# Mixer input of the 512-token segments: loaded by feature and normalised in place, instead of normalised by token and turned on TensorE

## The chip, the cores and the metric

The kernel runs on one core of one Trainium2 chip. The metric is device time in microseconds (us) of that core for one launch; three runs of the kernel before are given. All arithmetic on the path that matters here is float32.

A reminder of the engines, in the names that the profile uses: PE is TensorE (its weight loads are listed as PEld), DVE is VectorE, ACT is ScalarE, POOL is GpSimd, SP is SyncE, which here issues DMAs. Each engine executes its own list of instructions strictly in order, and an instruction that waits holds up everything behind it on that engine.

## The reference, cut to what matters

The input is four sequences of 1024 tokens with 256 features. A Mamba-2 mixer and a gated feed-forward block follow each other, each with a layer norm in front of it and behind it:

```python
x = x + _layernorm(_mamba2_forward(_layernorm(x), ...))      # x: (4, 1024, 256)
x = x + _layernorm(_ffn(_layernorm(x), ...))

def _layernorm(x, axis=-1, eps=1e-05):
    m = jnp.mean(x, axis=axis, keepdims=True)
    v = jnp.var(x, axis=axis, keepdims=True)
    return (x - m) / jnp.sqrt(v + eps)

# inside the mixer the first use of its input u = _layernorm(x) is
zxbcdt = u @ in_proj_kernel          # (256 -> 1288): z, xBC and dt
```

The change concerns only the first layer norm, that of the mixer's input, and the form in which it reaches the first product. TensorE contracts over partitions, so that product wants the normalised input with its 256 features on partitions and the tokens along the row.

## The kernel before, in words

**Segments.** The tokens are cut into nine segments, `SEGS`: the first 256 and the next 256 tokens of sequence 0 (segments 0 and 1), then the first 512 tokens of sequences 1 to 3 (segments 2 to 4), then the last 512 tokens of all four sequences (segments 5 to 8). For each segment `mixer(s)` gives a list of steps (`norm_in`, `step_sizes`, `features` or `feature_pair`, `decays`, `gate` or `gate_pair`, and for every chunk of 128 tokens `inner`, `scan`, `gated`, `way_out`, `turned`), and `ffn(s)` gives those of the feed-forward block. From segment 2 on (feed-forward) and segment 4 on (mixer, `SEVEN`) the large products are done as seven half-size products on sums of operands.

**Order.** Nothing is issued directly. A `Recorder` notes each operation as a step with its operands, the bytes that it reads and writes and an estimated duration (`weigh`). `Recorder.issue` then plays the whole program through, engine by engine, with due times: of the steps whose inputs and buffers are due it takes the one with the lowest rank (`rank`), and writes the instructions in that order. So the order of all engines follows from estimates made on the host, and a changed step moves others far away from it. A small DMA (under 20,000 bytes) is due 1900 ns after its issue there, a large one by its bytes; whatever another engine takes from a DMA is planned 1500 ns later still (`LATE_DMA`).

**Buffers.** `pools` hands out slots by name. What matters here: `x` (input rows by token, three slots), `xn` (one chunk of normalised rows, two slots), `xnT` (the normalised input by feature, 128 partitions x 2 x 512, a single slot), `th` (128 x 512, three slots, otherwise used for the tanh in the convolution), `a`, `f` and `d` (banks of PSUM, where products land), `mvm` (mean and variance per token) and `rsm` (the reciprocal standard deviation).

**The step that is changed.** `norm_in` has the rows of the segment in `x`, 128 tokens on partitions, four chunks. DVE takes `bn_stats` and `bn_aggr` of each chunk; POOL makes (variance + eps) to the power of -0.5 in two instructions (`rstd_of`). Then for each chunk DVE writes (x - mean) * rstd into `xn`, and PE turns its two halves of 128 features with a product against the identity into two banks. Two copies on ACT move the banks to `xnT`. Those lines are:

```python
for i in range(NC):
    xn = get("xn")
    r.vector.tensor_scalar(xn, x[:, i, :], mv[:, i, 0:1], rs[:, i : i + 1], ALU.subtract, ALU.mult)
    for kk in range(2):
        r.tensor.transpose(pT[kk][:, i * P : (i + 1) * P], xn[:, kk * P : (kk + 1) * P], ident)
for kk in range(2):
    r.scalar.copy(xnT[:, kk, :], pT[kk][:, :T])
```

**What comes behind it.** `step_sizes` is the first reader of `xnT` on PE (eight small products with `dtw`), `input_sums` takes sums of its quarters on DVE (segments 4 to 8), `feature_pair` and `gate_pair` read it to the end of the mixer's projections. `pair` puts two results into two `f` banks, and `convolve` then reads each of them with one ACT instruction and three DVE instructions (the taps) before the bank is free again.

**DMA traffic next to it.** All large DMAs go through SP's one queue: the feed-forward weights in blocks of 1792 KB (`wide<-stock`, `fetch`), the mixer's weights of 448 KB (`win<-mstock`), decays that are written to DRAM and read back for many partitions at once (`rows<-cst`, then `e<-rows` and `r<-rows`), rows of the input (`x<-in_u`) and of the output (`out_dram<-fo`).

Of the kernel before, what the change touches and what calls it, by code (L numbers as in the profile page):

```python
# [14 lines left out]
ALU = mybir.AluOpType  # L15
PSUM = bass.MemoryType.PSUM

P = 128
EPS = 1e-5
NB, L, DM = 4, 1024, 256  # L20
DI, NH, HD, DS = 512, 8, 64, 128
# [7 lines left out]
CMAX = TMAX // P  # L29
# [376 lines left out]
def mamba_ffn_kernel(  # L406
    ctx: ExitStack,
    tc: tile.TileContext,
    u: bass.AP,
    w_in: bass.AP,  # L410
    conv_w: bass.AP,
    conv_b: bass.AP,
# [13 lines left out]
    r = Recorder(tc.nc)  # L426
    sb = ctx.enter_context(tc.tile_pool(name="sb", bufs=1))
    psum = ctx.enter_context(tc.tile_pool(name="psum", bufs=1, space=PSUM))
    hbm = ctx.enter_context(tc.tile_pool(name="hbm", bufs=1, space=bass.MemoryType.DRAM))

    def pool(name, shape, k=1, ahead=2, of=None, dtype=F32):
        of = of or sb
        return Pool([of.tile(shape, dtype, name=f"{name}{j}") for j in range(k)], ahead)

    def fixed(name, shape, dtype=F32):
        return pool(name, shape, dtype=dtype).get()

    def given(ap):
        return Pool([ap]).get()

    u, w_in, conv_w, conv_b, dt_bias, a_log, d_skip, norm_w, w_out = map(
        given, (u, w_in, conv_w, conv_b, dt_bias, a_log, d_skip, norm_w, w_out))
    g_pack, g_scale, u_pack, u_scale, d_pack, d_scale, out = map(
        given, (g_pack, g_scale, u_pack, u_scale, d_pack, d_scale, out))

# [9 lines left out]
        "yo": pool("yo", [P, DI // P, P]), "xf": pool("xf", [P, 2, P], 2),  # L455
        "xfT": pool("xfT", [P, 2, TMAX], 2), "act": pool("act", [P, HALF], 3, 3),
        "fo": pool("fo", [P, DM], 2), "cst": pool("cst", [CMAX * NH, P], 2),
        "rows": pool("rows", [CMAX * NH, P], 2, of=hbm), "dec": pool("dec", [P, 3 * CMAX * NH], 2),
        "edge": pool("edge", [P, NF, 3], 2), "part": pool("part", [P, NF, 3], 2),
        **{k + who: pool(k + who, shape, 4, 4) for who in "mf"  # L460
           for k, shape in (("mv", [P, CMAX, 2]), ("st", [P, 6]), ("rs", [P, CMAX]))},
# [5 lines left out]
    def get(tag):  # L467
        return pools[tag].get()


    def rows_of(s):
        b, t0, T = SEGS[s]
        return b * L + t0, T
# [3 lines left out]
    def by_segment(s, tag, cut):  # L477

        if s > 1:
            return cut(get(tag), slice(0, SEGS[s][2]))  # L480
        if tag not in shared:
            shared[tag] = get(tag)
        return cut(shared[tag], slice(SEGS[s][1], SEGS[s][1] + SEGS[s][2]))

    xs = {}
# [11 lines left out]
    def load_win(c0, c1, queue=r.sync):  # L497
# [8 lines left out]
                     in_=w_in[:, DPROJ - NH :].rearrange("(k p) m -> p k m", p=P))  # L506
# [3 lines left out]
    for name, shape, src in (("dtb", [P, NH], dt_bias), ("aneg", [P, NH], a_log),  # L510
                             ("cw", [P, NF, 4], conv_w), ("cb", [P, NF], conv_b),
                             ("dsk", [P, DI // P], d_skip), ("nw", [P, DI // P], norm_w)):
        t = small_loads[name] = fixed(name, shape)
# [14 lines left out]
    mhalf = fixed("mhalf", [P, CMAX])  # L528
# [55 lines left out]
    def little(tag, n):  # L584
        return get(tag)[:, :n]

    def rstd_of(var, n, factor=1.0):

        v = get("rsm")[:, :n]
        r.gpsimd.tensor_scalar(v, var, factor, EPS * factor, ALU.mult, ALU.add)  # L590
        r.gpsimd.tensor_tensor(v, v, mhalf[:, :n], ALU.pow)
        return v

    def stats_of(rows, who="m"):

        n = len(rows)
        mv = get("mv" + who)[:, :n, :]
        for i, row in enumerate(rows):
            st = get("st" + who)
            r.vector.bn_stats(st, row)  # L600
            r.vector.bn_aggr(mv[:, i, :], st)
        return mv
# [133 lines left out]
    def mixer(s):  # L736


        b, t0, T = SEGS[s]
        NC = T // P  # L740
        W = NC * NH
        v_ = {}

        def ps_a():

            v_["n"] = v_.get("n", 0) + 1
            if s == 0:
                return (banks_a if v_.get("out") else banks_f).get()
            return (banks_d if s == 1 and v_["n"] % 2 else banks_a).get()

        def norm_in():
            x = v_["x"] = xs[s]
            mv = stats_of([x[:, i, :] for i in range(NC)])
            rs = rstd_of(mv[:, :, 1], NC)
            xnT = v_["xnT"] = by_segment(s, "xnT", lambda t, c: t[:, :, c])
            pT = [ps_a() for kk in range(2)]
            for i in range(NC):
                xn = get("xn")
                r.vector.tensor_scalar(xn, x[:, i, :], mv[:, i, 0:1], rs[:, i : i + 1],
                                        ALU.subtract, ALU.mult)  # L760
                for kk in range(2):
                    r.tensor.transpose(pT[kk][:, i * P : (i + 1) * P],
                                        xn[:, kk * P : (kk + 1) * P], ident)
            for kk in range(2):
                r.scalar.copy(xnT[:, kk, :], pT[kk][:, :T])
# [307 lines left out]
        def way_out(i):  # L1073

            x, y = v_["x"], v_["y", i]

            v_["out"] = OUT and i == NC - 1
            pr = ps_a()  # L1080
            for c in range(4):
                r.tensor.matmul(pr[:, :DM], lhsT=y[:, c, :], rhs=wo[:, c, :],
                                 start=(c == 0), stop=(c == 3), skip_group_check=True)
            r.tensor.matmul(pr[:, DM : DM + 1], lhsT=v_["sz"][:, 0, i * P : (i + 1) * P],
                             rhs=ones[:, 0:1], start=False, stop=True, skip_group_check=True)
            q = v_["q", i] = get("one")
            r.vector.tensor_scalar(q, pr[:, DM : DM + 1], EPS / DI, 4 * EPS * EPS, ALU.mult, ALU.add)
            so = get("one")
            junk = get("xn")
            r.scalar.activation(junk, pr[:, :DM], AF.Square, scale=1.0 / math.sqrt(DM),  # L1090
                                 accum_out=so)
            r.gpsimd.tensor_tensor(q, q, so, ALU.add)
            r.gpsimd.tensor_tensor(q, q, mhalf[:, 0:1], ALU.pow)
            r.vector.scalar_tensor_tensor(x[:, i, :], pr[:, :DM], q, x[:, i, :],
                                           ALU.mult, ALU.add)


            mv = stats_of([x[:, i, :]])
            rs = rstd_of(mv[:, :, 1], 1, 2.0 ** -12)
            xf = v_["xf", i] = get("xf")  # L1100
            r.vector.tensor_scalar(xf, x[:, i, :].rearrange("p (j two) -> p two j", two=2),
                                    mv[:, 0, 0:1], rs, ALU.subtract, ALU.mult)

        def turned(i):
# [3 lines left out]
            for kk in range(2):  # L1108
                r.tensor.transpose(pfT[:, kk * P : (kk + 1) * P], v_["xf", i][:, kk, :], ident)
            r.scalar.copy(xfT[s][:, :, i * P : (i + 1) * P],  # L1110
                           pfT[:, : 2 * P].rearrange("p (k t) -> p k t", k=2))

        steps = [norm_in, step_sizes]
        if s >= SEVEN:
            steps += [input_sums, lambda: (carried(), feature_pair(4)), decays,
# [8 lines left out]
        for j in range(NC + 4):  # L1124
            for d, stage in enumerate((inner, scan, gated, way_out, turned)):
                i = j - d
# [145 lines left out]
    prepare_small()  # L1272
    ns = len(SEGS)
    mix = [mixer(s) for s in range(ns)]

    def do(kind, s, steps):
# [98 lines left out]
```

## Time and profile before

| | |
|---|---|
| three runs, us | 1000.05, 999.85, 998.04 |
| median, us | 999.85 |
| profiled execution, first to last instruction (span), us | 995.4 |
| median of the runs less that span, us | 4.45 |
| granted TensorE clock | 0.999 |
| PE busy | 983.0 us (99%), 5275 matmuls |
| DVE, ACT, POOL busy | 650.1 us (65%), 517.0 us (52%), 305.1 us (31%) |
| DMA | 111.76 MB, mean 112 GB/s |

The profile is of one execution. Its own time as a whole is not listed apart from the runs; its span leaves out what lies before the first and after the last instruction, and 4.45 us is the distance of the median from it. A float32 matmul appears as two records, and its listed duration runs to the modelled end of its pipeline, so neighbours overlap: what an instruction costs on PE is read from the distance of one start to the next. In the profile all instructions of the program carry one line, L379, that of the helper which issues the recorded steps, so they are told apart by the names of the buffers: `a<-ident,xn` is a turn of normalised rows, `xnT<-a` the copy behind it.

### The profile page before, as it was taken

How to read it: one execution, taken by the hardware profiler on the slowest of the kernel's cores; microseconds unless marked ns; L12 is line 12 of the kernel's file. 1: busy time of each engine (PE TensorE's matmuls, PEld its weight loads, DVE VectorE, ACT ScalarE, POOL GpSimd, SP SyncE). 2: the span in 40 equal slices, each digit the busy share in tenths (PEclk: the TensorE clock that was granted, in tenths of full speed). 3: DMA queues.
4: the chain of work that ended last, by engine and by line, in shares of the span. 5: the costliest groups of instructions: out<-in, count | busy, mean ns of one | idle time of the engine just before them, and what ended most of it. 6: DMA issues, size and time to landing. Idle time of an engine off the chain costs nothing.

```text
span 995.4 us, 14948 instructions
## 1 busy us (share of the span) xinstructions
PE 983.0 (99%) x5275; PEld 813.7 (82%) x5275; DVE 650.1 (65%) x1412; ACT 517.0 (52%) x1289; POOL 305.1 (31%) x491
## 2 busy tenths in 40 slices
PE   8999999999999999999999999999999999999998
PEld 6788777877788878888888888888888888888886
DVE  4998576568666967787678754777467874432431
ACT  5645865447564764576457733576236762321321
POOL 2836654821250335024502431034310452001001
PEclk9999999999999999999999999999999999999999
DMA  6542153424423422354144423244233322422310
GB/s 203 110 112 91 78 167 117 170 64 139 163 76 98 131 81 92 127 159 156 43 145 142 157 75 106 91 136 153 76 116 132 98 102 96 148 74 95 107 43 21
DMA packets 48659, 111.76 MB, mean 112 GB/s; under 512 B 4664, under 2 KB 35768, under 8 KB 44472
## 3 DMA queue, kind: packets, MB, share of 16 engines
q1 hardware_dynamic: 48008, 110.78, 33.8%
q8 instruction: 41, 0.67, 0.3%
q14 instruction: 34, 0.28, 0.1%
q10 hardware_dynamic: 576, 0.02, 0.0%
HBM read 96.83 MB, written 13.96 MB: 111 GB/s over the span
## 4 chain that ended last, share of the span: by engine, by line
PE 94%; DVE 2%; POOL 1%; ACT 1%; issue 1%; POOLq 0%; DVEq 0%; ACTq 0%
PE f L379 48%; PE a L379 23%; PE d L379 23%; DVE xc L379 1%; DVE y L379 0%; DVE wide L379 0%; POOL sz L379 0%; ACT big L379 0%; DVE xn L379 0%; POOL y L379 0%; POOL rsf L379 0%; DVE yo L379 0%; POOL wd L379 0%; DVE e L379 0%; DVE big L379 0%
## 5 line engine op out<-in xcount | busy, mean ns | idle before, releaser
L379 PE MATMUL f<-wide 128*128 128x256 f32 x880 | 250.1, 382 | 0.1
L379 PE MATMUL f<-xfT,wide 128*128 128x256 f32 (+1 forms) x1024 | 248.4, 356 | 0.3 <-ACT big L379 0.2
L379 PE MATMUL d<-wd,big 128*128 128x256 f32 x992 | 248.0, 380 | 0.0
L379 PEld LDWEIGHTS d<-wd,big 128*128 128x128 f32 x992 | 183.6, 190 | 26.9 <-issue 4.1
L379 PEld LDWEIGHTS f<-xfT,wide 128*128 128x128 f32 x1024 | 171.2, 191 | 26.3 <-issue 5.9
L379 PEld LDWEIGHTS f<-wide 128*128 128x128 f32 x880 | 157.5, 190 | 32.2 <-issue 5.0
L379 DVE TENSOR_TENSOR f<-f,sums 128x256 f32<-128x256 f32 x216 | 92.4, 430 | 100.0 <-PE f L379 92.2
L379 POOL TENSOR_SCALAR_AFFINE_SELECT e<-e 128x1024 f32<-128x1024 f32 x31 | 35.3, 1137 | 201.5 <-DMA e<-rows 201.5
L379 ACT COPY f<-f 128x256 f32<-128x256 f32 x129 | 46.4, 362 | 93.0 <-PE f L379 70.4
L379 ACT ACTIVATE big<-f 128x512 f32<-128x512 f32 x108 | 63.1, 598 | 52.3 <-DVE f L379 40.8
L379 DVE TENSOR_TENSOR big<-big,f 128x512 f32<-128x512 f32 x108 | 73.2, 684 | 13.2 <-PE d L379 4.9
L379 ACT ACTIVATE e<-e,ncs 128x128 f32<-128x128 f32 x248 | 77.7, 392 | 5.2 <-POOL e L379 5.1
L379 DVE SCALAR_TENSOR_TENSOR xc<-f,cw,xc 128x511 f32<-128x511 f32 (+5 forms) x102 | 70.6, 713 | 1.8 <-ACT tail L379 0.4
L379 ACT ACT_TABLE_LOAD x52 | 66.7, 1283 | 4.3 <-issue 2.7
L379 PE MATMUL f<-xnT,win 128*128 128x256 f32 x240 | 66.1, 382 | 0.0
L379 POOL TENSOR_SCALAR rsf<-rsf 128x1 f32<-128x1 f32 x32 | 6.2, 193 | 187.1 <-ACT act L379 186.0
L379 PE MATMUL a<-wo,y 128*128 128x256 f32 x240 | 57.1, 381 | 0.0
L379 POOL TENSOR_TENSOR sz<-sz 128x256 f32<-128x256 f32 (+1 forms) x64 | 39.5, 619 | 35.5 <-ACT sz L379 34.2
L379 PEld LDWEIGHTS a<-wo,y 128*128 128x128 f32 x240 | 45.0, 190 | 6.3 <-DVE mvm L379 0.3
L379 PEld LDWEIGHTS f<-xnT,win 128*128 128x128 f32 x240 | 44.0, 190 | 7.2 <-ACT bt L379 0.8
L379 POOL TENSOR_TENSOR state<-state,dec 128x512 f32<-128x512 f32 x24 | 25.2, 1049 | 80.7 <-PE a L379 69.7
L379 DVE SCALAR_TENSOR_TENSOR fo<-d,rsf,x 128x256 f32<-128x256 f32 x30 | 14.3, 480 | 52.3 <-POOL rsf L379 52.2
(273 smaller groups left out, 1543.7 us busy)
## 6 DMA issues: line engine op xcount, KB each, us to landing
wide<-stock SPq DMA_DIRECT2D x28, 1792.0 KB, 7.3
e<-rows SPq DMA_DIRECT2D x31, 512.0 KB, 4.1
win<-mstock SPq DMA_DIRECT2D x25, 448.0 KB, 3.4
r<-rows SPq DMA_DIRECT2D x56, 128.0 KB, 4.6
stock<-sums SPq DMA_DIRECT2D x8, 512.0 KB, 2.6
out_dram<-fo SPq DMA_DIRECT2D x30, 128.0 KB, 1.7
x<-in_u_dram SPq DMA_DIRECT2D x7, 512.0 KB, 4.2
stock<-wide SPq DMA_DIRECT2D x6, 512.0 KB, 6.4
```

What stands on the lines that cost most here:

```text
L379: getattr(getattr(self.nc, st.queue), st.name)(*[real(a) for a in st.args], **{k: real(a) for k, a in st.kwargs.items()})
```

## The change

For segments 2 to 8 `norm_in` hands over to a new function, `norm_turned`; segments 0 and 1 stay as they are. The kernel gets one more input, `u_t`, the same rows of `u` stored by feature (256 x 4096; laid out with the other inputs, ahead of the launch). The rows by token are still loaded into `x`, for the statistics and for the residual. `xnT` is loaded from `u_t` by one DMA of 512 KB. The means and the reciprocal deviations, which stand one token per partition, are written to a row of 512 numbers in DRAM each (`lines`, 4 bytes at a time), and each row is read back into all 128 partitions (`th`). POOL then subtracts the row of means from `xnT` in place, and DVE multiplies by the row of reciprocal deviations in place, each as one instruction over 128 x 1024.

```diff
+        "lines": pool("lines", [2, CMAX * P], 2, of=hbm),
...
-    def rstd_of(var, n, factor=1.0):
+    def rstd_of(var, n, factor=1.0, to=None):
         v = get("rsm")[:, :n]
+        to = to or v
         r.gpsimd.tensor_scalar(v, var, factor, EPS * factor, ALU.mult, ALU.add)
-        r.gpsimd.tensor_tensor(v, v, mhalf[:, :n], ALU.pow)
-        return v
+        r.gpsimd.tensor_tensor(to, v, mhalf[:, :n], ALU.pow)
+        return to
...
+        def norm_turned():
+            x = v_["x"] = xs[s]
+            r0, _ = rows_of(s)
+            mv = stats_of([x[:, i, :] for i in range(NC)])
+            rstd_of(mv[:, :, 1], NC, to=mv[:, :, 1])
+            xnT = v_["xnT"] = get("xnT")
+            r.sync.dma_start(out=xnT,
+                             in_=u_t[:, r0 : r0 + T].rearrange("(k p) t -> p k t", p=P))
+            lines = get("lines")
+            for k, op in enumerate((ALU.subtract, ALU.mult)):
+                r.sync.dma_start(out=lines[k].rearrange("(i p) -> p i", p=P), in_=mv[:, :, k])
+                by_token = get("th")
+                r.sync.dma_start(out=by_token, in_=lines[k].partition_broadcast(P))
+                (r.vector if k else r.gpsimd).tensor_tensor(
+                    xnT, xnT, by_token.unsqueeze(1).to_broadcast([P, 2, T]), op)
+
         def norm_in():
+            if s > 1:
+                return norm_turned()
...
+        ("u_t", g["L0_attn_u"].reshape(NB * L, DM).T),
```

## The prediction

> **What bounds the kernel now.** I read the page's busy lines, its slices and its chain first. The numbers behind "PE" are busy time, share of the span and instructions; a 9 in the slices means 90% busy or more.
>
> ```profile
> PE 983.0 (99%) x5275; PEld 813.7 (82%) x5275; DVE 650.1 (65%) x1412; ACT 517.0 (52%) x1289; POOL 305.1 (31%) x491
> PE   8999999999999999999999999999999999999998
> PEclk9999999999999999999999999999999999999999
> PE 94%; DVE 2%; POOL 1%; ACT 1%; issue 1%; POOLq 0%; DVEq 0%; ACTq 0%
> ```
>
> PE is the bound from end to end, at full clock, and 94% of the chain that ended last is PE itself. So time is won by taking instructions from PE, and lost by whatever makes PE wait, since its list is executed in order.
>
> Next the timeline around the turns of segment 8 (columns: start, length, engine, operation):
>
> ```profile
> 735.53 0.36 PEld L379 LDWEIGHTS a<-ident,xn 128*128 128x128 f32 x2
> 735.74 0.38 PE L379 MATMUL a<-ident,xn 128*128 128x128 f32 x2
> 735.96 0.60 PE L379 MATMUL f<-wide 128*128 128x256 f32 x2
> 736.39 0.38 PE L379 MATMUL a<-ident,xn 128*128 128x128 f32 x2
> 736.61 0.60 PE L379 MATMUL f<-xfT,wide 128*128 128x256 f32 x2
> ```
>
> Two turns take 0.22 us from start to start (735.74 to 735.96), so one costs 0.11 us, not its listed length. One full product (two matmuls of 256 columns) takes 0.43 us (735.96 to 736.39). The turns stand between products without a gap: they are on the path.
>
> Then the groups by shape, for prices (count, busy us, mean ns, idle before):
>
> ```profile
> L379 DVE TENSOR_SCALAR xn<-x,mvm,rsm 128x256 f32<-128x256 f32 x32 | 13.6, 435 | 5.5 <-POOL rsm L379 2.8 <-PE a L379 2.3 <-ACT xn L379 0.3
> L379 ACT COPY xnT<-a 128x512 f32<-128x512 f32 x14 | 7.7, 590 | 8.2 <-PE a L379 8.2
> L379 DVE TENSOR_TENSOR e<-e,a 128x1024 f32<-128x1024 f32 x28 | 34.0, 1216 | 3.7 <-ACT e L379 3.1 <-ACT bt L379 0.4
> L379 POOL TENSOR_TENSOR y<-xc,dsk 128x512 f32<-128x512 f32 x32 | 32.7, 1039 | 34.5 <-PE a L379 18.4 <-DVE xc L379 11.1 <-PE f L379 4.9
> L379 POOL TENSOR_TENSOR y<-y,yo 128x512 f32<-128x512 f32 x28 | 36.0, 1285 | 2.8 <-DVE yo L379 2.6
> L379 POOL TENSOR_TENSOR rsm<-rsm,mhalf 128x4 f32<-128x4 f32 x7 | 7.2, 1034 | 0.3
> L379 DVE SCALAR_TENSOR_TENSOR xc<-f,cw,xc 128x511 f32<-128x511 f32 x30 | 22.4, 745 | 0.9
> ```
>
> Last the DMA issues (count, KB each, median us from issue to landing), and SP's timeline:
>
> ```profile
> wide<-stock SPq DMA_DIRECT2D x28, 1792.0 KB, 7.3
> e<-rows SPq DMA_DIRECT2D x31, 512.0 KB, 4.1
> out_dram<-fo SPq DMA_DIRECT2D x30, 128.0 KB, 1.7
> rows<-cst SPq DMA_DIRECT2D x7, 16.0 KB, 1.4
> dtw<-in_w_in_dram SPq DMA_DIRECT2D x1, 8.0 KB, 3.8
> 759.34 0.32 SPq L379 DMA_DIRECT2D wide<-stock  x1
> 760.72 0.32 SPq L379 DMA_DIRECT2D rows<-cst  x1
> 768.62 0.32 SPq L379 DMA_DIRECT2D e<-rows  x1
> ```
>
> `rows<-cst` usually lands in 1.4 us. Behind a 1792 KB block it did not: its reader `e<-rows` was issued 7.9 us later. A small DMA behind a weight block waits for the block.
>
> **The change, part by part.** The sum is made on the profiled execution (span 995.4 us) and carried to the median, 999.85, with the 4.45 us between them unchanged.
>
> *Removed from PE:* 8 turns in each of 7 segments, 56 x 0.11 = 6.1 us, all on the path. That is the whole possible gain by arithmetic.
>
> *Removed elsewhere:* 28 `xn` on DVE (28 x 0.435 = 12.2 us) and 14 copies on ACT (14 x 0.59 = 8.3 us). Both engines are a third idle or more; I count nothing, as PE's work covers them.
>
> *Added to DVE:* 7 multiplications over 128x1024, at 1.22 us by `e<-e,a`, 8.5 us. Less than was removed; the cost lies in its waits, below.
>
> *Added to POOL:* 7 subtractions over 128x1024, 2 x 1.04 = 2.1 us each by `y<-xc,dsk` (also a repeated operand), at most 2 x 1.285 = 2.6 us by `y<-y,yo`. POOL is 31% busy; nothing for its time, but it lies in the chain below.
>
> *Added to SP:* five DMAs per segment. `xnT<-u_t` stands 44 to 79 us of PE work ahead of the first product that reads it in segments 3 to 8, so its landing (4.1 us, same size as `e<-rows`) is covered. In segment 2 it stands 3.3 us ahead of the subtraction; the multiplication is 3.6 us further, so 4.1 + 2.1 us are nearly covered: nothing, with 0 to 3 us as ends (landing 4.1 to 7.3).
>
> *The new chain, per segment.* From the start T of the first POOL instruction: 0.19 + 1.03 us to the deviations; means in DRAM; means back on all partitions; subtraction; and beside them the deviations out and back; multiplication; first product. No row shows 512 runs of 4 bytes to DRAM. The nearest are `rows<-cst` (1.4 us, 32 runs) and `dtw` (3.8 us, 256 runs of 32 bytes, in the crowded start): I take 3.0, nearer to `dtw` for its many runs. The read-back of 256 KB lies between `out_dram<-fo` (128 KB, 1.7) and `e<-rows` (512 KB, 4.1): by size 2.5. Then means out 3.0, back 5.5, subtracted 7.6; deviations issued 1.3, out 4.3, back 6.8; multiplication from 7.7 to 8.9; about 9.2 us with hand-offs, where the old chain took 7.9 (in segment 8 from that POOL instruction at 732.66 to the first `dtw` product at 740.60).
>
> How much work does the order put over it? Counted in the changed program's PE list between that POOL instruction and the first `dtw` product, at 0.43 us per product: 39.0, 13.3, 11.5, 11.1, 10.8, 15.1 and 15.1 us for segments 2 to 8. All exceed 9.2. The multiplication waits on DVE, and behind it stand the sums that the feed-forward products need, so its own place matters: in segments 4, 5 and 6 at 10.2, 9.2 and 9.1 us, against 7.7: covered. In segment 3 the deviations leave late (8.5), so 8.5 + 3.0 + 2.5 = 14.0 against 13.3: 0.7 late. In segments 7 and 8 a weight block is issued between the two lines, 1.55 us after T (732.66 to 734.21 in this trace); it lands in 8.0 us at that place, the deviations behind it at about 9.7, back 12.3, against 12.5: just covered. I take +1.0 us for all seven.
>
> The ends: below, 0, with 1.4 and 1.7 us. Above, with 3.8, 4.1 and 2.6 us: multiplication ready at 10.8 in segments 4 to 6 (0.6 + 1.6 + 1.7 late), 13.9 in 7 and 8 (1.4 each), 16.4 in 3 (3.1): 9.8 us.
>
> The Trainium skill, "DMA: Bandwidth & Descriptors", section Specifications, speaks against this step: below 512 bytes per descriptor the DMA engine reads, modifies and writes. No run here shows what that costs for 4 bytes. If it doubled the share of a line that its many runs make (3.0 less 1.4, an estimate from that page), both lines would land 1.6 us later: segment 3 late by 2.3, 5 and 6 by 0.3 together, 7 and 8 by 1.4 each, in all 5.4 us, and the sum would be 999.85 - 6.1 + 2.2 + 5.4 = 1001.4.
>
> *What the new order moves.* The planner's order changes nearly everywhere. I looked at the place where PE most easily runs dry: after a pair of feature blocks, the bank stays taken until ACT (0.78 us) and the taps have read it. In the order before, the PE work between a pair's last product into a bank and the next use of that bank is never under 4.3 us, and its trace shows no such wait above 0.5 us after the start. In the order after, one place, the last pair of mixer 5 (near 420 us), has 2.6 us: five products and the bank's own. To be covered there: ACT 0.78, the three added columns 0.2, four taps (one of the other bank in between) 4 x 0.745 = 3.0, an ACT copy 0.36, hand-offs 0.3, together 4.6 to 4.8. So PE waits 2.2 us (ends 0 and 3: earlier work may already be late, or DVE may be). All other places have 4.5 us or more: nothing.
>
> Sum: -6.1 + 1.0 + 2.2 = -2.9 us, 999.85 - 2.9 = 996.95, so 997.0.
>
> **The rivals.**
>
> *Slower: the lines are late.* One mechanism, the two 4-byte lines in DRAM; place, DVE's in-order list in segments 3 to 8; price, each late microsecond holds the sums of the feed-forward products and so PE. It decides from about 2.9 us of lateness in all, half a microsecond per segment, and costs up to 9.8: 999.85 - 6.1 + 2.2 + 9.8 = 1005.8; its middle, 7 us, gives 1003. For it: nothing in the trace writes runs this short, and `rows<-cst` shows that small DMAs are delayed by others. Against: five of the seven covers have a microsecond or more to spare.
>
> *No change.* Lateness of 3 to 6 us eats the gain: 998 to 1001.8. For it: the margins in segments 3, 7 and 8 are under a microsecond.
>
> *The full gain.* No lateness, and the gap in mixer 5 is filled because PE runs later against DVE than the plan has it: 999.85 - 6.1 = 993.75. For it: PE waits little before, so the planner's estimates hold. Against: that bank's chain is in the order itself.
>
> *PE's time is not the bound*, and the turns were free: 999.85 + 2.2 + 1.0. The timeline speaks against it, as each pair of turns pushes the next product by 0.22 us.
>
> **How the numbers follow.** Chances: the forecast, -2 to -5 us, 0.40; the full gain 0.12; no change within 2 us 0.20; late lines, slower by over 2 us, 0.28 (turns that were free are in these last two). 0.2% is 2.0 us, which is also the spread of the three runs, 998.04 to 1000.05. So faster 0.52, same 0.20, slower 0.28. The range for 8 in 10 starts just under the full gain, 993.0, and reaches to the middle of the late lines, 1003.5; the likeliest case alone is 995 to 998.
>
> **What would show it.** Right: 56 turns fewer, PE busy shorter by about 6 us, one PE wait of some 2 us near 420 us behind a convolution's taps, and `lines` landing in about 3 us. The step on the lines is wrong if DVE's multiplication waits for a DMA by over a microsecond in several segments; the step on the order is wrong if PE shows no wait near 420 us, or others of that size. The whole is wrong if PE's idle time grows by more than 6 us.

## The result, and the profile after

The changed kernel took 1078.49 us (median, 1076.17 to 1083.0), the kernel before, beside it, 999.89 us: a ratio over all runs of 1.0795, 95% interval 1.0768 to 1.0822. The forecast was 997.0 us, with a range up to 1003.5. The sign was wrong, and so was the size.

The page of the changed kernel, its busy lines, its slices and its chain:

```profile
PE 998.1 (93%) x5219; PEld 820.7 (76%) x5219; DVE 652.6 (61%) x1391; ACT 514.5 (48%) x1279; POOL 320.4 (30%) x498
PE   8999999689995997899979999699996999999998
PEclk8999999989997999799989999899998999999999
PE 81%; DMA 11%; DVE 4%; POOL 2%; issue 2%; ACT 0%; ACTq 0%; SPq 0%; POOLq 0%; DVEq 0%
```

There are 56 products fewer, as intended, yet PE's busy time grew from 983.0 to 998.1 us, and the span outside it from 12.4 to 76.3 us. The row of nines has six clear dents, and at each one the row of the granted clock dips too. DMA, absent from the chain before, is 11% of it; the same chain by lines gives 8% to the writing of the lines alone.

The waits of PE, then those of POOL and DVE for the lines read back, then SP's own for the lines written (total us, times, longest us):

```profile
PE a L379 <- DVE xnT L379: 50.2, 6, 13.4
PE a L379 <- DVE xf L379: 6.1, 1, 6.1
PE f L379 <- DMA wide<-stock: 6.0, 2, 3.3
PE f L379 <- ACT f L379: 2.5, 2, 2.3
POOL xnT L379 <- DMA th<-lines: 65.4, 6, 19.5
DVE xnT L379 <- DMA th<-lines: 55.7, 5, 17.3
SPq L379 <- DMA lines<-mvm: 97.0, 12, 11.3
```

PE waits six times for the normalised rows and twice for a weight block. The wait for `xf` (the normalised input of the feed-forward block) is one for a line too: in segment 5 POOL's subtraction waits 7.1 us for the means, and behind it in POOL's list stands the reciprocal deviation that `xf` needs. The fourth line, with 2.3 us at the longest, is the dry bank of mixer 5 that the forecast named. The DMA issues of the same kernel (count, KB each, median us from issue to landing):

```profile
lines<-mvm SPq DMA_DIRECT2D x14, 2.0 KB, 10.5
th<-lines SPq DMA_DIRECT2D x14, 256.0 KB, 4.4
```

A line of 2 KB takes 10.5 us by the median, more than the 7.1 us of a weight block of 1792 KB in the same kernel. Here is one segment in full, the eighth: SP's timeline, then the chain of waits over the same stretch (start, length, what), then PE's timeline:

```profile
800.34 0.38 SPq L379 DMA_DIRECT2D lines<-mvm  x1
801.95 0.33 SPq L379 DMA_DIRECT2D wide<-stock  x1
802.37 0.39 SPq L379 DMA_DIRECT2D lines<-mvm  x1
809.61 0.32 SPq L379 DMA_DIRECT2D th<-lines  x1
```

```profile
802.37 18.62 DMA lines<-mvm
821.04 3.96 DMA th<-lines
825.09 1.24 DVE xnT L379
```

```profile
817.32 1.01 PE L379 MATMUL f<-xfT,wide 128*128 128x256 f32 x2 [3.31 <-DMA wide<-stock]
826.37 1.08 PE L379 MATMUL a<-xnT,dtw 128*32 128x128 f32 x16 [5.48 <-DVE xnT L379]
```

The means leave at 800.34, and only at 809.61 can SP issue their read-back: 9.3 us. The weight block issued 1.6 us after the means lands 15.2 us after its issue, where the kernel before showed 8.0 us at that place, and only then, at 817.32, does PE go on. The deviations, behind both, need 18.62 us. In the records of the 16 DMA engines, all 512 runs of 4 bytes start within the microsecond from 801; then 16 packets of the weight block start by 804, none from 804 to 807, and 8 from 807 to 811. Those first 16 packets take 4.4 to 9.7 us each, the later ones 0.54. So the short runs start at once and the block behind them is held up; that it is the completion of the short runs which holds it is my reading of these records.

### The profile page after: what moved, and what is told of

The parts are those of the page before. It is cut to its first block, busy times and chain, and to the rows that moved or that the text cites. A ratio compares the mean times of both kernels' runs of the same rounds, so it can differ in the third digit from the quotient of the medians.

```text
span 1074.4 us, 14896 instructions
## 1 busy us (share of the span) xinstructions
PE 998.1 (93%) x5219; PEld 820.7 (76%) x5219; DVE 652.6 (61%) x1391; ACT 514.5 (48%) x1279; POOL 320.4 (30%) x498
## 4 chain that ended last, share of the span: by engine, by line
PE 81%; DMA 11%; DVE 4%; POOL 2%; issue 2%; ACT 0%; ACTq 0%; SPq 0%; POOLq 0%; DVEq 0%
PE f L379 42%; PE a L379 20%; PE d L379 19%; DMA lines<-mvm 8%; DMA th<-lines 2%; DMA mstock<-sums 1%; DVE xc L379 1%; DVE xnT L379 1%; POOL sums L379 0%; DVE stm L379 0%; DVE f L379 0%; DVE y L379 0%; DVE wide L379 0%; POOL sz L379 0%; POOL one L379 0%
## 5 line engine op out<-in xcount | busy, mean ns | idle before, releaser
L379 PE MATMUL f<-wide 128*128 128x256 f32 x880 | 254.3, 388 | 3.0 <-ACT f L379 2.5
L379 PEld LDWEIGHTS d<-wd,big 128*128 128x128 f32 x992 | 186.1, 192 | 27.5 <-issue 3.8
L379 PEld LDWEIGHTS f<-xfT,wide 128*128 128x128 f32 x1024 | 174.6, 192 | 35.0 <-issue 13.6
L379 PE MATMUL f<-xnT,win 128*128 128x256 f32 x240 | 73.2, 411 | 0.1
L379 PEld LDWEIGHTS f<-xnT,win 128*128 128x128 f32 x240 | 47.1, 206 | 9.8 <-issue 1.6
L379 PE MATMUL a<-xnT,dtw 128*32 128x128 f32 x112 | 7.1, 400 | 50.2 <-DVE xnT L379 50.2
L379 POOL TENSOR_TENSOR y<-xc,dsk 128x512 f32<-128x512 f32 x32 | 32.7, 1039 | 64.6 <-DVE xc L379 39.9
```

What stands on the lines that cost most here:

```text
L379: getattr(getattr(self.nc, st.queue), st.name)(*[real(a) for a in st.args], **{k: real(a) for k, a in st.kwargs.items()})
```

## The experiments

Three theories were set against each other. **A**: the 4-byte runs of a line hold up the DMA engines for about 8 us each, and with them whatever is queued behind. **B**: the round trip through DRAM is late whatever its runs. **C**: the work in place on POOL and DVE and the new order cost the time. Runs e1 to e4 had the kernel before at 999.39 us, e5, e8, e9 and e10 at 999.45, e11 to e14 at 998.83; every ratio below is to the kernel before in the same group, with its 95% interval.

**e1_runs512B.** The order of the changed kernel on every engine; only what a line's write copies is exchanged when it is issued.

```diff
+                st = r.sync.dma_start(out=lines[k].rearrange("(i p) -> p i", p=P), in_=mv[:, :, k])
+                st.instead = {"out": lines[k].rearrange("(i p) -> i p", p=128), "in_": ones[:4, :128]}
```

> Same order of instructions on every engine as in the changed kernel, same DMAs, same bytes; only the 14 writes of the lines are in 4 runs of 512 bytes instead of 512 runs of 4 bytes. Their source is a fixed tile of ones, so the statistics are left out of the result, and the write no longer waits for them. Theory A (runs of 4 bytes to DRAM: each line holds the DMA rings for about 8 us): lines land in under 3 us, PE waits for DVE's xnT by under 5 us in all instead of the 50 us listed, time 996 to 1001. Rival B (the round trip through DRAM, whatever the runs): lines still land in 8 us or more, time above 1060. Rival C (the in-place work on POOL and DVE and the new order): lines are quick and the time stays above 1040.

Measured: 1001.07 us, ratio 1.0015 (1.0006 to 1.0025). All waits for `xnT` are gone, and with this exchange 77.4 of the 78.6 us went. So neither the round trip by itself (B) nor the work in place and the order (C) makes up the loss. What is left shows the price of the order. The largest wait of PE (of those the order before does not have) and, behind it, a table of stretches (length, busy us and count of PE, PEld, DVE, ACT and POOL, then the granted clock):

```profile
PE f L380 <- ACT f L380: 2.5, 2, 2.3
442.70:446.20 3.50, 3.50 (x10) 2.24 (x9) 1.89 (x4) 0.90 (x2) 1.37 (x2) 0.51 0.02 7
446.20:449.60 3.40, 3.40 (x19) 2.57 (x18) 3.16 (x7) 1.73 (x4) 1.66 (x2) 1.00 0.00 0
```

The dry bank of mixer 5 is where it was forecast, with 2.3 us waited and 2.46 us lost from start to start. Behind it PE ran 3.41 us at half clock, 10 products in the time of 19, which costs another 1.7 us. Two places that I had counted at nothing (`a<-ident,xf` near 305 and 503 us, both behind DVE) lose 1.3 and 1.2 us. Together 6.7 us, of the 7.8 by which this run lies above the full gain (999.39 less 6.1). So even with lines in time this order of the instructions would not have been faster. One thing is not clean here: the exchanged write does not wait for the statistics either, which the fifth run takes up.

**e2_fixed.** The lines travel as in the changed kernel, but POOL and DVE read a fixed tile in place of `th`, so no engine waits for the lines.

```diff
+                st.instead = {0: by_piece, 1: by_piece,
+                              2: ones.unsqueeze(1).to_broadcast([P, 2 * T // P, P])}
```

> Same order, and the lines are written and read back as in the changed kernel, but POOL's subtraction and DVE's multiplication take a fixed tile of ones instead of the lines (the normalisation is left out of the result), so that nothing on an engine waits for them. Theory A (rings held by 4-byte runs): the waits for xnT go, but weight blocks and input rows queued behind the lines stay late, PE still waits for wide<-stock by 5 us or more; time 1000 to 1020. If the lines cost only by the wait of their readers and hold up nobody else: 994 to 999. Rival C (in-place work and order): above 1040.

Measured: 1027.18 us, ratio 1.0281 (1.0266 to 1.0296), above the range of theory A. The readers of the lines account for 51.3 us; 26 us over the 512-byte version remain with no reader. PE's waits name them: weight blocks of both kinds, and once a sum that ACT could make only when an output row had landed (in 4.75 us):

```profile
PE f L380 <- DMA wide<-stock: 8.9, 2, 4.9
PE f L380 <- ACT sums L380: 4.7, 1, 4.7
PE f L380 <- DMA win<-mstock: 4.4, 1, 4.4
```

**e3_turned.** The whole computation, with lines written in 8 runs of 512 bytes: PE turns the statistics (128 x 8 to 8 x 128, one product per segment), ACT copies them out of the bank. The order is planned anew.

```diff
+            pmv = ps_a()
+            r.tensor.transpose(pmv[: 2 * NC, :P], mv.rearrange("p i k -> p (i k)"), ident)
+            mvT = get("raw")[: 2 * NC, :]
+            r.scalar.copy(mvT, pmv[: 2 * NC, :P])
+            r.sync.dma_start(out=lines, in_=mvT)
```

> The whole computation. Means and deviations are first turned by one small product on PE (128 x 8 to 8 x 128) and copied by ACT, then written to DRAM as 8 runs of 512 bytes in one DMA; the rest as in the changed kernel; the order is planned anew. Theory A: lines land in 1.4 to 2.5 us, time 994 to 1001, so that the gain of the removed turns shows or nearly so. Rival B: lines land in 8 us or more, time above 1050. Rival C: above 1040 with quick lines.

Measured: 1016.66 us, ratio 1.0182 (1.0162 to 1.0202), a miss for theory A's figure: the lines are no longer late (PE's wait for `xnT` is 1.0 us in all), but between 100 and 400 us PE stands idle for 13.0 us, where the kernel before shows 1.4, in waits of up to 2.1 us behind ACT and DVE. Whether the turn's bank and copy or only the newly planned order costs this was not separated.

**e4_planned.** The 4-byte runs stay; the planner is told that a line holds the DMA engines for 8 us.

```diff
+                elif st.shapes[0] == (P, CMAX):
+                    wires = max(free[e], wires) + 8000.0
+                    st.end = wires + 1700.0
```

> The changed kernel, with one line of its planner altered: a line's DMA is due 9.7 us after its issue and holds the wires for 8 us, instead of 1.9 us and nothing. Lines still have 4-byte runs. Theory A says that the lateness hurts only because the order doesn't cover it: other products are put over it, PE waits for xnT by under 15 us in all, time 1000 to 1020. If the single xnT buffer leaves no work to put there, the time stays above 1050.

Measured: 1039.91 us, ratio 1.0385 (1.0333 to 1.0438). The wait for `xnT` fell to 0.3 us as expected, the time did not fall to 1020: PE now waits in small pieces elsewhere (`xf` 7.7 us, `f` 3.6, and more below 3). An order planned around the lines halves the loss and no more.

**e8_runs4B_fixed.** The partner of the first run: the same exchange, but 512 runs of 4 bytes.

```diff
+                st.instead = {"in_": ones[:, :CMAX]}
```

> The changed kernel, in its own order on every engine, with the 14 writes of a line still as 512 runs of 4 bytes, but taken from the fixed tile `ones`, so that no write waits for the statistics (the statistics are left out of the result). It is the partner of the 512-byte version, from which it differs in the length of the runs alone. Theory A (the 4-byte runs hold the DMA rings for about 8 us a line): 1070 to 1080 us, as the changed kernel. Theory B (in the 512-byte version it was the removed wait for the statistics that brought the time back): about 1001 us. The line should take about 10 us to land.

Measured: 1051.73 us, ratio 1.0523 (1.0492 to 1.0553). Both theories miss. PE's waits and the landing:

```profile
PE a L380 <- DVE xnT L380: 39.2, 6, 15.3
lines<-ones SPq DMA_DIRECT2D x14, 2.0 KB, 12.3
```

Between this run and the first only the length of the runs differs (and with it their number, as a line has 2 KB in both), so that is worth 50.7 us by itself. The other 26.8 us, up to the changed kernel, come with writes that can leave only after the statistics; that a late line costs more the later it starts is the likely reason, not a measured one. The line lands no sooner than in the changed kernel.

**e5_runs16B.** 128 runs of 16 bytes, otherwise as the first run (`ones[:128, :4]` as the source).

> As the 512-byte version, in the same order, with each line written as 128 runs of 16 bytes from the fixed tile (the statistics are left out). Theory A with a price for each run, from 10.5 us for 512 runs against 1.4 to 2 us for a few: about 16 to 18 ns a run, so 128 runs should hold the rings for some 2 to 2.5 us and land in 3.5 to 4.5 us: with covers of 10.8 to 15.1 us the lines are then nearly on time, 1001 to 1008 us. If instead the price goes with a run being shorter than 512 bytes at all (a fixed penalty for each line), the time stays at 1060 to 1080.

Measured: 1004.84 us, ratio 1.0050 (1.0015 to 1.0085); one wait for `xnT` of 2.7 us is left. The time is as a price per run has it; a fixed penalty for being under 512 bytes is out.

The landing, 7.0 us by the median, is longer than the 3.5 to 4.5 us expected, but these medians hold the time behind other transfers too. SP's list gives a cleaner price: the second line of segments 3 to 5 is issued when the first has landed, and SP then waits for it before it issues the read-back. In segment 4, with 4, 128 and 512 runs (e1, this run, e8):

```profile
291.69 0.32 SPq L380 DMA_DIRECT2D lines<-ones  x1
294.17 0.32 SPq L380 DMA_DIRECT2D th<-lines  x1
296.17 0.42 SPq L380 DMA_DIRECT2D lines<-ones  x1
300.19 0.32 SPq L380 DMA_DIRECT2D th<-lines  x1
315.89 0.61 SPq L380 DMA_DIRECT2D lines<-ones  x1
326.90 0.32 SPq L380 DMA_DIRECT2D th<-lines  x1
```

Over the three segments that is 2.3 to 2.5 us for 4 runs of 512 bytes, 3.1 to 4.0 us for 128 of 16 bytes and 10.1 to 11.0 us for 512 of 4 bytes. With 16 bytes a line is as quick as expected. Whether it is the number of runs that costs or their being as short as 4 bytes can't be told apart, since every line has 2 KB.

**e14_fixed_noreadback.** As e2_fixed, with the read-backs taken from a row of the turned input, so that SP does not wait for a line either.

```diff
+                st.instead = {"in_": u_t[k, r0 : r0 + T].partition_broadcast(P)}
```

> As the fixed-tile version (lines written in 4-byte runs from the statistics, POOL's subtraction and DVE's multiplication read the tile `ones`), in the same order, with one thing more: the two broadcast reads of a line take a row of the turned input instead, so nothing at all waits for a line's landing, not even SP's own list. The normalisation is left out of the result. Two causes of the fixed-tile version's 27 us are told apart. If the 4-byte writes hold the DMA rings, the weight blocks and x rows behind them stay late and the time stays near 1027 us (1020 to 1030). If it was SP, which issues in order and stood 107 us before the read-backs, the blocks leave in time and the time falls to 1000 to 1006 us.

Measured: 1017.81 us, ratio 1.0195 (1.0179 to 1.0211), between the two expectations: both causes exist. SP's stand before the read-backs (107 us in all in e2) was worth 9.4 us of e2's time, and 16.7 us over the 512-byte version remain where nothing waits for a line. What waits is what was queued behind it:

```profile
PE f L380 <- DMA wide<-stock: 8.0, 2, 4.1
th<-in_u_t_dram SPq DMA_DIRECT2D x14, 256.0 KB, 9.1
```

Beside each of the two waits for a block stands a stretch at half clock, 6.8 and 3.4 us. (The 16.7 us are an upper figure for the writes alone, since the writes of the 512-byte version also leave earlier.) And a broadcast that lands in 4.4 us when it is issued after its line takes 9.1 us when issued behind one still under way. Whether the lines would spare the blocks if they were sent through a queue of their own was not tried.

**e9_dve.** The whole computation, with no turn on PE: DVE transposes the statistics in blocks of 32 x 32 and four DMAs write 32 runs of 128 bytes.

```diff
+            raw = get("raw")
+            r.gpsimd.memset(raw[:, 2 * NC : 32], 0.0)
+            mv = raw[:, : 2 * NC].rearrange("p (k i) -> p i k", k=2)
...
+            r.vector.transpose(raw[:, 32:64], raw[:, :32])
...
+            for g in range(0, P, 32):
+                r.sync.dma_start(out=lines[:, g : g + 32], in_=raw[g : g + 2 * NC, 32:64])
```

> The whole computation. The statistics are turned by one 32x32 transpose on DVE, so a line leaves as runs of 128 bytes: four DMAs of 8 runs each write means and deviations together, and two broadcasts read them back. PE has no turn at all. The order is planned anew. Theory A: the lines land in 1.5 to 3 us and no multiplication waits; the time is that of the 512-byte version with its order's own losses, 995 to 1005 us. Theory C (the work in place on POOL and DVE behind the lines costs whatever the runs are): 1010 or more, with waits of PE for xnT.

Measured: 1003.56 us, ratio 1.0036 (1.0020 to 1.0053). PE waits for `xnT` four times, 5.8 us in all, the longest 1.9: small lateness, as theory A expects, but not none.

**e10_dve_replanned, e11_before_replanned, e12_dve_replanned2, e13_dve_replanned3.** The same instructions in other orders: the versions that turn on DVE under three other sets of planner constants, and the kernel before under the first of these sets. That of e12:

```diff
-LATE_PE, LATE, LATE_DMA = 75.0, 100.0, 1500.0
-HOLD = 300.0
+LATE_PE, LATE, LATE_DMA = 100.0, 60.0, 1500.0
+HOLD = 200.0
...
-            return (260 if n < 40 else 150 + n * (1.66 if st.repeats else 2.1)), 100.0
+            return (260 if n < 40 else 150 + n * (1.9 if st.repeats else 2.1)), 100.0
...
-                    st.end = wires + 1700.0
+                    st.end = wires + (2200.0 if st.repeats else 1700.0)
...
-... 10 * s - 10, "w": WEIGHTS + 10 * s, ...
+... 10 * s - 11, "w": WEIGHTS + 10 * s, ...
```

> The kernel that turns the statistics on DVE, with four constants of the planner changed (allowance between engines 60 instead of 100 ns, for a DMA 1800 instead of 1500, for holding an activation table 200 instead of 300, a higher price for POOL's repeated operand, and the mixer's rank two places earlier), so that its order is another one with the same instructions. If what is left against the kernel before lies in the order (places like the bank of mixer 5), the time moves by several us against its partner, and may fall to 992 to 998 us, the full gain of 6.1 us being the floor. If the order does not matter, both are within 2 us of each other.

> The kernel before, whole, with the same four constants of the planner changed as in the second version that turns the statistics on DVE (and the same rank). No instruction is added or removed; only the order differs. It shows what another order of the same work is worth by itself: if orders of this kernel differ by less than 2 us, 998 to 1002 us; if several us are in it, 992 to 998 or 1002 to 1008, and what is left of the 6.1 us in the versions with 128-byte runs is not to be read from one order alone.

> The whole computation, statistics turned on DVE, a third order (allowances 100, 60 and 1500 ns, table hold 200 ns, a broadcast priced half a microsecond later, POOL's repeated operand dearer, the mixer's rank one place earlier). The floor is the full gain, 993.8 us; the default order gave 1003.6 and the second 999.8. By the theory that only places like a dry bank or a late line are left, 994 to 1001 us with PE waits for xnT of under 3 us; by the theory that the in-place work always costs what the turns did, 999 to 1004.

> As the last, a fourth order (allowances 100, 60 and 1500 ns, a broadcast priced a whole microsecond later, patience 45 instead of 30 ns). The broadcasts land after 3.6 us where the plan had 2.9, so this order should have no PE wait for xnT: 994 to 1001 us by the first theory, 999 to 1004 by the second.

Measured: e10 999.83 us, ratio 1.0014 (0.9995 to 1.0034); e11 1004.07, 1.0066 (1.0047 to 1.0084); e12 993.83, 0.9958 (0.9942 to 0.9974); e13 995.69, 0.9968 (0.9956 to 0.9980). So another order of the same instructions moves the kernel before by 5 us, and the versions that turn on DVE by almost 10. e12 and e13 are the two that beat both kernels; e12's lead, 5.0 us by the medians and 4.2 (2.6 to 5.8) by the ratio, is most of the 6.1 us that the turns were worth. It is the best of four orders, though, and the kernel before was run in two. The busy line and the chain of its page, and PE's only wait for the normalised rows:

```profile
PE 979.2 (99%) x5219; PEld 808.0 (81%) x5219; DVE 655.9 (66%) x1398; ACT 505.2 (51%) x1271; POOL 323.1 (33%) x505
PE 94%; DVE 2%; DMA 1%; ACT 1%; POOL 1%; issue 0%; ACTq 0%; SPq 0%; POOLq 0%; DVEq 0%
PE a L379 <- DVE xnT L379: 0.5, 1, 0.5
```

PE is 94% of the chain again, and 0.5 us of waiting for `xnT` is all there is in the whole run. The theory that the work in place always costs what the turns did is out. Whether the kernel before would gain from the constants of e12 or e13 was not tried; under the one set that both have, that of e10 and e11, the version that turns on DVE is ahead by 4.2 us by the medians, and under the constants of the changed kernel (e9 against the kernel before) it is behind by 4.1. So what part of the lead is the change's and what part the order's stays open.

## Why the prediction was wrong, and where it was right

*Removed from PE*: right. 56 products are gone, and in the versions with lines in time PE's turns take 6.1 to 6.2 us less, measured from start to start. PE's busy time as a whole fell by 3.8 us in e12.

*Added to DVE and POOL*: right in DVE for the time of the work, a little low in POOL. Of the groups of the changed kernel (count, busy us, mean ns, idle before):

```profile
L379 POOL TENSOR_TENSOR xnT<-xnT,th 128x1024 f32<-128x1024 f32 x7 | 16.4, 2340 | 65.6 <-DMA th<-lines 65.4 <-DVE state L379 0.2
L379 DVE TENSOR_TENSOR xnT<-xnT,th 128x1024 f32<-128x1024 f32 x7 | 8.8, 1258 | 62.9 <-DMA th<-lines 55.7 <-POOL xnT L379 7.2
```

2.34 us against 2.1 (inside the bound of 2.6), 1.26 against 1.22. The idle column beside them is where the forecast fell. "Nothing" for POOL was wrong in another way: POOL's list is in order as well, and a subtraction that waits holds the work behind it. In segment 5 it waited until 426.05 us; DVE waited 6.8 us for POOL before it could make `xf`, and PE 6.1 us for `xf`.

*The new chain per segment*: this is the step that failed, in the term "means out 3.0", whose upper bound was 3.8. It measured 10.5 us as a median; in segment 8 the means took 9.3 us and the deviations, behind a weight block, 18.62. The bound came from `dtw`, which has 256 runs of 32 bytes and is read from DRAM, not written to it. But the length of the runs and their number are what differed, and a row with runs eight times as long bounds nothing. For "+1.0, ends 0 to 9.8" of lateness the lines cost 77.4 us with all that follows from them (e1), 50.7 of it by the length of the runs alone (e8). Two further assumptions in the same step failed with it. I let a late line cost only its own lateness at the multiplication, and did name that a small DMA waits behind a weight block; that a weight block waits behind a small DMA I did not consider, and it is worth up to 16.7 us with nobody waiting for the line (e14), 26 us with SP waiting (e2). And I counted no price behind a wait. In the changed kernel the clock records show half clock for 68 us after the start (the last section has more on it). PE is busy for 42.7 us of the stretches at half clock, the one at the start included; half of that, about 21 us, less the 6.1 of the turns, is the 15.1 us by which its busy time rose.

The rival "lines are late" had the right mechanism and place, and the wrong price (1005.8 at most), because it took the same two bounds. (By the prediction's own terms, 6.1 less 2.2, the sign changes at 3.9 us of lateness, not 2.9, and 998 to 1001.8 us belong to 2 to 6 us, not 3 to 6; and its 10.8 us for segments 4 to 6 add up to 10.6. None of this bears on the miss.) The sentence from the Trainium skill, "DMA: Bandwidth & Descriptors", section Specifications, pointed the right way. The estimate made from it, 5.4 us of lateness, was as far off as the rest: it doubled a share that was itself read from longer runs. Its limit of 512 bytes by itself does not describe what was seen: 128-byte runs (e12) and 16-byte runs (e5) came within 0.5% of the kernel before, 4-byte runs did not.

*What the new order moves*: right in its place, too small in its size. The dry bank of mixer 5 cost 2.3 us of wait as counted (2.2), but 4.2 in e1 with the half clock behind it, and two other places 2.5 us where I had "nothing". The term was 6.7 us in place of 2.2 in e1, so the forecast would have missed by sign even with lines in time: e1 is 1001.07, not 996.95. In the changed kernel itself the same gap had no half clock behind it.

*xnT by feature*: the load was covered, as said; PE, POOL and DVE show no wait of note for it in the changed kernel.

Of the tells, two spoke at once: DVE's multiplication waited for a DMA in five segments, 55.7 us, and PE's idle time grew by 64 us where 6 was the limit.

## What to carry to other kernels

Before statistics or any column of single numbers is sent through DRAM, count the runs of the write, not its bytes: 512 runs of 4 bytes took longer to land than a weight block, and the weight blocks and broadcasts issued behind them came late, whether anybody waited for the line or not. Turn the column on chip first; a 32 x 32 transpose on DVE did it here for 0.2 us. A bound taken from the nearest row is only a bound if that row has the property in doubt, and when a gain is under 1% of the time the planner's new order has to be measured beside it, since the order alone moved the kernel before by 5 us and the version that turns on DVE by almost 10.

## What the runs showed of the hardware that was not expected

**A wait shorter than 3.41 us can halve the clock, and its length does not decide it.** The granted clock was either 1.0 or 0.5, and its stretches at 0.5 were multiples of 3.41 us (3.41, 6.83, 10.24, 13.65), apart from the last of each trace, which ends with it. Within a trace they also begin on one grid of that step: in e1 at 19.51, 53.65 and 442.77 us, 10 and then 114 steps apart. A gap of 2.46 us was followed by such a stretch in e1, and one of 2.85 us in e5, while gaps of 1.75 us (e14) and of 2.1 us (e9) were not. But the very same gap of 2.46 us, at the dry bank of mixer 5, was followed by one in e1, e5, e8 and e14 and by none in the changed kernel and e2, and in e4 a gap of 1.8 us (it ends at 219.62) was followed by one.

Where the gap lies on the grid seems to count. In e1 it lies between two lines of the grid (439.6 to 442.0, lines at 439.36 and 442.77), and in e14 as well. In the changed kernel a line falls into it (485.0 to 487.5, line at 486.41), and in e2 (454.6 to 457.1, line at 456.35). In e8, though, a line falls into the gap too, at 472.38, and the stretch came; so the rule stays open.

The Trainium skill, "TensorE: Matmul & The Clock Gate", Part 1, gives a window of 3413 ns and two settings of the clock gate, half and full, which agrees with these records; its condition of at least one idle window of about 3.4 us does not cover the gap of 2.46 us, and here the measurement decides.

**DVE's transpose.** This is its row in e12 (the 128 x 32 statistics of one segment):

```profile
L379 DVE STREAM_TRANSPOSE raw<-raw 128x32 f32<-128x32 f32 x7 | 1.4, 202 | 0.4 <-POOL raw L379 0.4
```

It takes 0.2 us per segment, 1.4 us in all, and lets the lines leave in runs 32 times as long.
